# A third early block of deformable samples, a denser second layer, and an addition and a copy on other engines

## The chip, the core and the metric

The kernel runs on one core of one Trainium2 chip. The metric is the time of one execution on the device, in microseconds, as the median of several runs.

## The reference, cut to what matters

Four layers are computed in turn on an input of 2 images (batches) of 256 channels and 64 x 64 pixels:

```
x = attention(group_norm(x)): 4 heads, q.k over all 4096 pixels, softmax, times v,
    projection, plus the normalized x
x = x + position term
x = bottleneck(x): 1x1 convolution to 64 channels, deformable 3x3 convolution
    (offsets and a mask from a 3x3 convolution; each of 9 taps is a bilinear
    sample at its own place), 1x1 convolution to 256 channels, plus x
x = x + two times: group_norm, relu, deformable 3x3 convolution over 256 channels
    (offsets from a 7x7 depthwise and a 1x1 convolution)
```

A bilinear sample is a gather of four neighbouring pixels, weighted. Everything is float32.

## The kernel before, in words

The pixels of a batch are tiled into 8 blocks of 512 (`NB`). The order of the work on TensorE, ScalarE, VectorE and GpSimd (POOL in the profile) is the order in which the program issues it; the DMAs of SyncE (SP) are placed by the framework. The program has two parts.

**Attention** (line 181 on) goes through 4 units, a batch and a pair of heads each. A unit has 16 blocks of 256 queries, a block 16 positions `n`, so there are 1024 positions; the main loop (line 677) makes two of them per turn. For each it multiplies queries and keys (line 580), takes the maxima on VectorE (592), the exponentials on ScalarE (598), turns them on TensorE (610), copies the turned halves out of PSUM on VectorE or ScalarE (`keep`, line 617) and multiplies with the values (639). At the end of a block the softmax shares of its parts are turned and sent through DRAM (`spread`, line 499: a store to `share_d` and two loads of `f`), and GpSimd merges the parts with them (`combine`, 514). The next block's first product is copied into the same tile `o` (471).

What else is to be done runs in the background, as generators. `background(count)` (line 661) goes down their list and makes up to `count` productive steps. It is called for each position that has no step of the attention's own (`small`, 691) and once more at the end of a turn (724). The list holds, in turn: the bottleneck's first layer and offsets (`before`, 954); for batch 0 within units 2 and 3 its second layer (`conv`, 1041), which has 144 steps of two gathers on POOL, a product on VectorE (1065) and two additions (1075, 1076; on POOL for batch 0, on VectorE for batch 1), with transposes, matmuls and copies between; then `early_image` (1178), which normalizes the result and writes the image `img3` that deform gathers from; and in unit 3 `early_samples` (1215). The latter computes the offsets for the first `EARLY` blocks of deform. Each block has 36 gathers (9 taps, 4 groups of 128 pixels); `gather` (1254) issues them one by one on POOL, 11 per 16 positions, and stores each gathered tile of 128 x 1024 to `samp_d` by SP.

**Deform** (line 1299) computes both deformable layers of both batches: 4 x 8 blocks of 36 steps `s`. A step gets its gathered tile (`gather`, 1437, called 8 steps ahead), weighs its first corner on ScalarE (1459), adds the other three on VectorE (1465), turns the sample on TensorE (1477), and every four steps it is copied (1486) and multiplied (1496). For the first `EARLY` blocks of batch 0 the tiles are read from `samp_d` by SP (the first 8 by POOL) and no offsets are computed; for all others POOL gathers.

Beside the steps run `Side` generators with a rate of calls per step: the second layer of batch 1 (`seconds`, 0.9 a step and 2.5 more for each step of the early blocks), after its end the image of batch 1 (0.9 a step; it first loads batch 1 by SP into the memory that the second layer used), and the offsets of later blocks (24 per 36 steps, begun 58 steps before block `EARLY`):

```
offs = [Side(EARLY * BLOCK - LEAD - 6, OFFS / BLOCK, begun)]
seconds = Side(0, 0.9, second, lambda s: 2.5 * min(s, EARLY * BLOCK))
```

`corners` (731) turns offsets into indices and weights with small VectorE operations; its tiles come from the pool that it is given.

Of the kernel before, what the change touches and what calls it, by code (L numbers as in the profile page):

```python
# [11 lines left out]
F32 = mybir.dt.float32  # L12
BF16 = mybir.dt.bfloat16
I32 = mybir.dt.int32
# [6 lines left out]
P = 128  # L21
# [4 lines left out]
K2 = 9  # L26
EPS = 1e-5
DWK = 7

EARLY = 2  # L30


GH, GW = H + 1, W + 2
# [31 lines left out]
class Net:  # L65
# [115 lines left out]
    def attention(self, bott):  # L181
# [4 lines left out]
        tc, nc, a = self.tc, self.nc, self.a  # L186
        with ExitStack() as ctx:
# [58 lines left out]
            q, k, v = {}, {}, {}  # L246
# [370 lines left out]
            def keep(n, pts, engine):  # L617

                u, i, c, t, h = parts(n)
                if n % 4 == 0 and n // 4 not in ets:  # L620
                    ets[n // 4] = etp.tile([P, 8, 2, 256], F32, name="et")
                for j, pt in enumerate(pts):
                    at = P * t + 64 * j
                    dst = ets[n // 4][:, :, h, at : at + 64]
                    if j and (u < 2 or h == 0 or t):
                        if engine == "DVE":
                            nc.vector.tensor_copy(dst, pt)  # L627
                    elif engine == "ACT":
                        nc.scalar.copy(dst, pt)  # L629
# [31 lines left out]
            def background(count):  # L661
                for g in list(back):
                    while count:
                        r = next(g, None)
                        if r is None:
                            back.remove(g)
                            break
                        if not r:
                            break
                        count -= 1  # L670
# [6 lines left out]
            while n < last + 4 or back or more or any(own.values()):  # L677
                u, d = divmod(n, per_unit)
                if d == 0 and u < len(units):
                    plan_unit(u)  # L680
                    if u == 0:
                        back.append(prepare(1))
                    if u == 1:
                        back.append(bott.before(0, bt, ps))
                    if u == 2:
                        back.append(first_batch())
                    if u == 3:
                        back.insert(0, bott.before(1, bt, ps))
                        back.append(self.early_samples(bott, bt, held, xp, vp, kp, ps))

                def small(at):
                    steps = own.pop(at, ())
                    for f in steps:
                        f()
                    if not steps and u > 1:
                        background(1)

                if n - 1 in pts:
                    p = pts.pop(n - 1)
                    keep(n - 1, p, "ACT")  # L700
                    keep(n - 1, p, "DVE")
                ps.flush()
                sc = [scores(m) for m in (n + 2, n + 3) if m < last]
                for m in range(len(sc)):
                    lowest(n + 2 + m, sc[m])
                if n < last:
                    p = turn(e.pop(n))
                    keep(n, p, "DVE")
                if sc:
                    e[n + 2] = exponentials(n + 2, sc[0])  # L710
                if n < last:
                    keep(n, p, "ACT")

                small(n)
                if 4 <= n < last + 4:
                    attend(n - 4)
                    attend(n - 3)
                small(n + 1)
                if n < last:
                    pts[n + 1] = turn(e.pop(n + 1))  # L720
                if sc:
                    e[n + 3] = exponentials(n + 3, sc[1])
                if u or n % 8 == 0:
                    background(1)

                for _ in range(1 + (n % 16 in (10, 12, 14))):
                    more = self.sample()
                n += 2


    def corners(self, i, pt, mask, base, idx, w4, pool):

        nc = self.nc
        p = pool.tile([P, 4, K2, 2], F32, name="pos")
        off = pt[:, :, 0 : 2 * K2].rearrange("p j (k t) -> p j k t", t=2)
        nc.vector.tensor_tensor(p, off, base[:, 4 * i : 4 * i + 4], ALU.add)
        if mask:
            mk = pool.tile([P, 4, K2], F32, name="mask")  # L740
            nc.vector.tensor_scalar_max(mk, pt[:, :, 2 * K2 : 3 * K2], -87.0)
        yield False
        if mask:

            nc.scalar.activation(mk, mk, AF.Exp, scale=-1.0)

        nc.vector.tensor_scalar(p, p, float(H), -1.0, ALU.min, ALU.max)
        whole = pool.tile([P, 4, K2, 2], I32, name="whole")
        nc.vector.tensor_copy(whole, p)
        yield True  # L750
        f = pool.tile([P, 4, K2, 2], F32, name="floor")
        nc.vector.tensor_copy(f, whole)
        g = pool.tile([P, 4, K2, 2], F32, name="above")
        nc.vector.tensor_tensor(g, f, p, ALU.is_gt)
        yield False
        nc.vector.tensor_tensor(f, f, g, ALU.subtract)
        nc.vector.tensor_scalar_min(f, f, float(H - 1))
        w = pool.tile([P, 2, 4, K2, 2], F32, name="wt")
        nc.vector.tensor_tensor(w[:, 1], p, f, ALU.subtract)
        yield False  # L760
        nc.vector.tensor_scalar(w[:, 0], w[:, 1], -1.0, 1.0, ALU.mult, ALU.add)
        at = pool.tile([P, 4, K2], F32, name="at")
        nc.vector.scalar_tensor_tensor(
            at, f[:, :, :, 0], float(GW), f[:, :, :, 1], ALU.mult, ALU.add
        )
        nc.vector.tensor_scalar_add(idx, at, float(GW + 1))
        yield True
        if mask:
            nc.vector.tensor_scalar_add(mk, mk, 1.0)
            nc.vector.reciprocal(mk, mk)  # L770
            yield False
            for s in range(2):
                nc.vector.tensor_mul(w[:, s, :, :, 1], w[:, s, :, :, 1], mk)
            yield False
        for s in range(4):
            nc.vector.tensor_mul(w4[:, :, :, s], w[:, s % 2, :, :, 0], w[:, s // 2, :, :, 1])
        yield True
# [76 lines left out]
    class Bottleneck:  # L854
# [44 lines left out]
        def pools(self, ctx, gathers=5):  # L899
            self.ahead = gathers - 1  # L900
            tc = self.net.tc
            return self.kept | {
                n: ctx.enter_context(tc.tile_pool(name=f"bt_{n}", bufs=bufs))
                for n, bufs in (("g", gathers), ("s", 8), ("t", 6), ("x", 2))
            }

        def block(self, pool, src, i):
# [133 lines left out]
        def conv(self, b, pools, ps):  # L1041
# [28 lines left out]
            def add(n, four, sampled):  # L1070

                i, g, js = steps[n]
                engine = (nc.gpsimd, nc.vector)[b]
                sm = pools["s"].tile([P, 2, CM], F32, name="bsmp")
                engine.tensor_add(four[:, :, 0:2, :], four[:, :, 0:2, :], four[:, :, 2:4, :])  # L1075
                engine.tensor_add(sm, four[:, :, 0, :], four[:, :, 1, :])
                if g < 4:
                    sampled.append(sm.rearrange("p n f -> p (n f)"))
                else:
                    sampled.extend(sm[:, m, :] for m in range(2))  # L1080
# [218 lines left out]
    def deform(self, bott):  # L1299
# [5 lines left out]
        with ExitStack() as ctx:  # L1305
            gp = ctx.enter_context(tc.tile_pool(name="df_g", bufs=10))
            wp = ctx.enter_context(tc.tile_pool(name="df_w", bufs=1))
            work = ctx.enter_context(tc.tile_pool(name="df_work", bufs=2))
            cp = ctx.enter_context(tc.tile_pool(name="df_c", bufs=4))
            sp = ctx.enter_context(tc.tile_pool(name="df_s", bufs=5))  # L1310
            tp = ctx.enter_context(tc.tile_pool(name="df_t", bufs=2))
            pmisc = ctx.enter_context(tc.tile_pool(name="df_pm", bufs=1, space=PSUM))
# [88 lines left out]
            def offsets(b, l):  # L1401
                if b == 0:
                    yield from offset_weights(l)
                wf = self.wf
                for i in range(EARLY if (b, l) == (0, 0) else 0, NB):
                    idx = cp.tile([P, 4, K2], I32, name="didx")
                    w4 = cp.tile([P, 4, K2, 4], F32, name="dw4")
                    corners[b, l, i] = idx, w4
                    yield from self.offsets(
                        i,  # L1410
                        [x[b][:, cb, :] for cb in range(2)],
                        lambda s, row: wf[:, s, DWK * row : DWK * row + DWK, :].rearrange(
                            "p t o -> p (t o)"
                        ),
                        self.vec[:, V_PWB + l : V_PWB + l + 1],
                        base, idx, w4, work, ods[i % 2], pd,
                    )

            ods = [wp.tile([P, 8, W + DWK - 1], F32, name=f"wide{n}") for n in range(2)]
# [284 lines left out]
```

## Time and profile before

| | us |
|---|---|
| median of 3 runs | 5151.03 |
| lowest and highest run | 5145.72, 5154.88 |
| span of the profiled execution, first to last instruction | 5149.0 |
| attention's units 0 to 3, from the first maximum of each | 59, 740, 1450, 2189 |
| deform's first weighed sample | 2995 |

The profiled execution is one run of its own. Its own time is its span, 5149.0 us, with what lies around the first and last instruction, which the profile doesn't give; the span lies within the range of the runs, 2.0 us under their median. The profile names an engine's work by line, tile and operation; a busy time is a union over instructions, and idle time is put down to what ended it.

### The profile page before, as it was taken

The numbers are of one execution on the slowest core, as the hardware profiler recorded it, in microseconds if no ns is written. First come the engines' busy times: TensorE is split into PE (matmuls) and PEld (weight loads), VectorE is DVE, ScalarE is ACT, GpSimd is POOL, SyncE is SP. The second block draws the span as 40 slices with busy tenths as digits, with TensorE's granted clock in tenths as the row PEclk, the third lists the DMA queues.
The fourth block names the chain that finished last, engine by engine and source line by source line (L and its number), as shares of the span: only waits on it lengthen the run. The fifth ranks groups of instructions, "written<-read, shape, count | busy, mean of one in ns | idle before, by whom it ended". The sixth has DMA issues, their size and how long they took to land. (4 is left out here: it accounts for less than half of the span.)

```text
span 5149.0 us, 100000 instructions
## 1 busy us (share of the span) xinstructions
PE 4816.8 (94%) x38200; PEld 2651.9 (52%) x38200; DVE 4196.7 (82%) x7929; ACT 2883.6 (56%) x5221; POOL 2254.7 (44%) x2256
## 2 busy tenths in 40 slices
PE   8999999999999999999999957679999999999998
PEld 5555565555565555565555523234444444444443
DVE  6878867878668888687766768878999999999998
ACT  5666656666666666666656622235444554454444
POOL 0111111111107777464023257775666566666665
PEclk9999999999999999999999967789999999999999
DMA  5231121111113333322557677679999999999998
GB/s 172 61 99 51 42 68 49 35 46 30 55 52 94 93 100 102 94 85 79 150 193 272 233 242 239 207 251 376 340 329 339 360 359 350 356 388 346 347 348 318
DMA packets 367022, 997.66 MB, mean 194 GB/s; under 512 B 61372, under 2 KB 98810, under 8 KB 366542
## 3 DMA queue, kind: packets, MB, share of 16 engines
q0 software_dynamic: 196560, 690.41, 37.7%
q1 hardware_dynamic: 169438, 300.73, 17.9%
q8 instruction: 300, 4.92, 0.4%
q14 instruction: 180, 1.47, 0.1%
q10 hardware_dynamic: 544, 0.13, 0.0%
HBM read 855.36 MB, written 127.35 MB: 191 GB/s over the span
## 5 line engine op out<-in xcount | busy, mean ns | idle before, releaser
L1465 DVE SCALAR_TENSOR_TENSOR smp<-four,dw,smp 128x256 f32<-128x256 f32 x3240 | 1503.8, 483 | 122.3 <-ACT smp L1459 44.4
L598 ACT ACTIVATE e<-sc,low 128x1024 f32<-128x1024 f32 x1024 | 1147.1, 1120 | 745.1 <-DVE low L592 741.4
L592 DVE TENSOR_REDUCE low<-sc 128x1 f32<-128x1024 f32 x1024 | 1204.8, 1218 | 228.1 <-PE sc L580 224.0
L846 POOL DMA_INDIRECT four<-img,didx x1080 | 1085.4, 1005 | 646.3 <-DVE smp L1465 349.2
L1496 PE MATMUL out<-st,wc 128*128 128x512 f32 x2304 | 1229.6, 616 | 65.0 <-ACT st L1486 33.6
L580 PE MATMUL sc<-k,qs 64*128 64x512 f32 x2048 | 997.1, 605 | 1.8 <-ACT e L598 1.4
L639 PE MATMUL av<-et,v 128*64 128x256 f32 x8192 | 996.5, 385 | 0.0
L580 PE MATMUL sc<-k,q 64*128 64x512 f32 x2048 | 977.3, 604 | 0.0
L519 POOL TENSOR_TENSOR o<-o,f 128x1024 f32<-128x1024 f32 x63 | 149.3, 2370 | 1771.5 <-DMA f<-share_d 890.1
L610 PEld LDWEIGHTS tt<-ident,e 64*128 64x128 f32 x16384 | 651.7, 139 | 519.3 <-issue 275.4
L1459 ACT ACTIVATE smp<-four,dw 128x256 f32<-128x256 f32 x1080 | 535.9, 507 | 594.3 <-PE pt L1477 460.4
L610 PE MATMUL tt<-ident,e 64*128 64x64 f32 x16384 | 726.1, 226 | 40.5 <-ACT et L629 19.9
L629 ACT COPY et<-tt 128x512 f32<-128x512 f32 x1152 | 659.5, 586 | 170.5 <-PE tt L610 169.2
L627 DVE COPY et<-tt 128x512 f32<-128x512 f32 x896 | 612.0, 683 | 161.3 <-PE tt L610 160.9
L639 PEld LDWEIGHTS av<-et,v 128*64 128x64 f32 x8192 | 552.1, 137 | 302.9 <-issue 48.4
L1477 PEld LDWEIGHTS pt<-ident,smp 128*128 128x128 f32 x2304 | 320.5, 144 | 740.8 <-issue 423.4
L846 POOL DMA_INDIRECT bfour<-img,bidx x576 | 581.0, 1009 | 184.2 <-issue 90.3
L1496 PEld LDWEIGHTS out<-st,wc 128*128 128x128 f32 x2304 | 392.0, 196 | 323.3 <-issue 216.5
L1477 PE MATMUL pt<-ident,smp 128*128 128x128 f32 x2304 | 454.6, 280 | 72.7 <-DVE smp L1465 67.1
L580 PEld LDWEIGHTS sc<-k,qs 64*128 64x128 f32 x2048 | 345.4, 188 | 215.7 <-issue 120.0
L1486 ACT COPY st<-pt 128x1024 f32<-128x1024 f32 x288 | 291.2, 1011 | 289.5 <-PE pt L1477 287.8
L803 PE MATMUL pd<-x,wf 128*126 128x512 f32 x840 | 433.4, 598 | 0.0
(183 smaller groups left out, 3600.4 us busy)
## 6 DMA issues: line engine op xcount, KB each, us to landing
f<-share_d SPq DMA_DIRECT2D x128, 256.0 KB
four<-samp_d SPq DMA_DIRECT2D x64, 512.0 KB
xb<-xn SPq DMA_DIRECT2D x55, 512.0 KB
img<-imgt SPq DMA_DIRECT2D x96, 256.0 KB
four<-img,didx POOLq DMA_INDIRECT x1080, 6.1
xa<-res SPq DMA_DIRECT2D x32, 512.0 KB
samp_d<-xb SPq DMA_DIRECT2D x32, 512.0 KB
xb<-in_x SPq DMA_DIRECT2D x20, 512.0 KB
```

What stands on the lines that cost most here:

```text
L580: nc.tensor.matmul(s[:, j, :], lhsT=q[u, i // 2][int(h != j)][halves[j], at : at + P], rhs=k[u][c][halves[j], h, :], start=True, stop=True,)
L592: nc.vector.tensor_reduce(low, s, AX.X, ALU.max, negate=True)
L598: nc.scalar.activation(e.rearrange("p j n -> p (j n)"), s, AF.Exp, bias=blk.low[:, g, c : c + 1], accum_out=blk.sum[:, g, c : c + 1],)
L610: nc.tensor.transpose(pt[:, m, :], e[half, m // 4, m % 4 * P : m % 4 * P + P], self.ident[half, half],)
L627: nc.vector.tensor_copy(dst, pt)
L629: nc.scalar.copy(dst, pt)
L639: nc.tensor.matmul(now["av"][halves[h], :], lhsT=v[u][c][:, m, halves[h]], rhs=ets[j][:, m, h, :], start=(m == 0), stop=(m == 7),)
L846: self.nc.gpsimd.indirect_dma_start(out=dst, out_offset=None, in_=img, in_offset=bass.IndirectOffsetOnAxis(ap=idx, axis=0),)
L1459: nc.scalar.mul(smps[s], fours[s][:, 0], weight(s, 0))
L1465: nc.vector.scalar_tensor_tensor(smps[s], four[:, c], weight(s, c), smps[s], ALU.mult, ALU.add)
L1477: nc.tensor.transpose(pts[u][:, c, j * P : (j + 1) * P], smp[:, c * P : c * P + P], self.ident,)
L1496: nc.tensor.matmul(outs[ob], lhsT=wc[k][:, c, ob * P : ob * P + P], rhs=sts[u][:, c, :], start=(k == 0 and c == 0), stop=(k == K2 - 1 and ...
```

## The change

`EARLY` becomes 3: a third block has its offsets computed, gathered and stored within the attention, and is read back in deform. In unit 2 one more of the turned halves' copies goes to ScalarE (positions with the second head and the second half of the queries; unit 3 is as it was). In units 2 and 3 every second turn makes two background steps at its end instead of one. The first of batch 0's two additions in the bottleneck's second layer is made on VectorE. To make room, `corners` uses one tile for three of its values, deform's corners come from a pool with one buffer, and the ring of bottleneck samples has 7 tiles instead of 8.

```diff
-EARLY = 2
+EARLY = 3
...
-                    if j and (u < 2 or h == 0 or t):
+                    if j and (u < 2 or h == 0 or t and u > 2):
...
                 if u or n % 8 == 0:
-                    background(1)
+                    background(1 + (u > 1 and n % 4 == 0))
...
-        whole = pool.tile([P, 4, K2, 2], I32, name="whole")
+        whole = pool.tile([P, 4, K2, 2], F32, name="whole").bitcast(I32)
...
-        g = pool.tile([P, 4, K2, 2], F32, name="above")
+        g = whole.bitcast(F32)
...
-        at = pool.tile([P, 4, K2], F32, name="at")
+        at = g.rearrange("p j k t -> p (j k t)")[:, : 4 * K2]
+        at = at.rearrange("p (j k) -> p j k", k=K2)
...
-                for n, bufs in (("g", gathers), ("s", 8), ("t", 6), ("x", 2))
+                for n, bufs in (("g", gathers), ("s", 7), ("t", 6), ("x", 2))
...
-                engine.tensor_add(four[:, :, 0:2, :], four[:, :, 0:2, :], four[:, :, 2:4, :])
+                nc.vector.tensor_add(four[:, :, 0:2, :], four[:, :, 0:2, :], four[:, :, 2:4, :])
...
+            once = ctx.enter_context(tc.tile_pool(name="df_k", bufs=1))
...
-                        base, idx, w4, work, ods[i % 2], pd,
+                        base, idx, w4, once, ods[i % 2], pd,
+                        odp=lambda: work.tile([P, 512], F32, name="od"),
```

## The prediction

> **What bounds the kernel now.** I read the page first, for the shape of the run.
>
> ```profile
> span 5149.0 us, 100000 instructions
> ...
> PE 4816.8 (94%) x38200; PEld 2651.9 (52%) x38200; DVE 4196.7 (82%) x7929; ACT 2883.6 (56%) x5221; POOL 2254.7 (44%) x2256
> ...
> POOL 0111111111107777464023257775666566666665
> ```
>
> TensorE is busy 94% on average, but the POOL slices show different stages. So I cut the span where they change. The columns are busy us (and instructions) of PE, PEld, DVE, ACT, POOL, then the granted clock, DMA share and GB/s.
>
> ```profile
> 1450.00:2189.00 739.00, 727.45 (x7908) 436.25 (x7906) 581.94 (x831) 493.02 (x920) 445.35 (x489) 1.00 0.31 90
> 2189.00:2975.00 786.00, 756.67 (x7865) 450.77 (x7863) 561.62 (x900) 509.63 (x947) 255.41 (x264) 0.99 0.50 166
> 3005.00:3300.00 295.00, 183.21 (x558) 84.57 (x559) 254.39 (x595) 66.60 (x123) 222.43 (x217) 0.75 0.72 234
> 3300.00:3460.00 160.00, 115.88 (x377) 55.11 (x376) 125.29 (x283) 46.49 (x82) 123.73 (x120) 0.84 0.70 223
> ...
> 3604.00:5100.00 1496.00, 1427.67 (x5123) 689.42 (x5122) 1401.55 (x3307) 737.07 (x1273) 935.66 (x934) 1.00 0.96 352
> ```
>
> Attention units 2 and 3 (first two rows) are TensorE's: 98% and 96% busy at full clock. Whatever is added to TensorE there is paid in full. From 3604 on, TensorE (95%), VectorE (94%) and the DMA engines (0.96) are all near their ends. In between, 3005 to 3460, nothing is full: TensorE 62%, VectorE 83%. The indirect gathers alone, by stage (POOL busy and count):
>
> ```profile
> 3005.00:3300.00 295.00, 222.43 (x217) 0.75 0.72 234
> 3300.00:3384.00 84.00, 64.80 (x64) 0.76 0.61 191
> 3384.00:3460.00 76.00, 58.93 (x57) 0.93 0.80 259
> ```
>
> 338 gathers in 455 us: one per 1.35 us, about 1.0 busy plus 0.3 to issue, evenly in every slice. POOL's issue is the limit of this stage, with VectorE close behind. Of the 338, 288 are second-layer gathers of batch 1 and the rest are deform's own. How many deform steps pass meanwhile is seen from ScalarE's first product (line 1459), one per step:
>
> ```profile
> 3384.00:3460.00 76.00, 14.90 (x30) 0.93 0.80 259
> 3460.00:3604.00 144.00, 37.56 (x76) 0.96 0.97 370
> 3604.00:3704.00 100.00, 31.56 (x63) 1.00 0.94 342
> ```
>
> With the steps before 3384 counted on the same line, deform stands at step 89 at 3384, at 119 at 3460 and at 195 at 3604. It then takes 1.59 us a step (57 us a block of 36).
>
> **Does the third block fit into attention?** I walked the background calls through the loop. Outside the unit changes, before makes 33 productive calls per 32 positions in unit 2 and after 41. Batch 0's second layer starts near position 546 in both and drains at 842 before, 780 after. The early image follows (852 to 886 before, 786 to 804 after). 72 gathers ran from position 902 to 1004; 108 would run from 812 to 968. The trace agrees for before: first such gather at 2614 us, last at 2913, attention's last exponential ends at 2966.8. So three blocks end 56 positions ahead of the end: no tail is added.
>
> **Attention, part by part.**
>
> *Third offset block.* Two blocks' matmuls in attention:
>
> ```profile
> L803 PE MATMUL pm<-v,bx 128*126 128x512 f32 (+3 forms) x56 | 23.3, 573 | 0.0
> ...
> L823 PE MATMUL pm<-k,shift 126*32 126x512 f32 x28 | 3.9, 602 | 0.0
> L837 PE MATMUL pm<-sel,bst 128*128 128x32 f32 x16 | 2.2, 279 | 0.0
> ```
>
> 29.4 us for two, so +14.7 us on a full TensorE. Removing it from deform saves nothing by itself: block 2's offsets lie in the POOL-limited stage.
>
> *36 more gathers, stores and the SP queue.* A store of samples waits on SP for its gather, and the shares that the attention's merge needs stand behind it:
>
> ```profile
> 2790.38 6.23 SPq L1259 DMA_DIRECT2D samp_d<-xb  x3
> 2792.32 0.27 DVE L504 COPY shares<-pm 16x128 f32<-16x128 f32 x1
> ...
> 2799.20 0.38 SPq L506 DMA_DIRECT2D share_d<-shares  x1
> ...
> 2808.57 2.34 POOL L519 TENSOR_TENSOR o<-o,f 128x1024 f32<-128x1024 f32 x1 [21.27 <-DMA f<-share_d]
> ...
> 2813.08 0.42 DVE L471 COPY o<-av 128x256 f32<-128x256 f32 x1 [6.17 <-POOL avs L525]
> ...
> 2814.16 1.03 PE L610 MATMUL tt<-ident,e 64*128 64x64 f32 x15 [4.55 <-DVE et L627]
> ```
>
> The shares were ready at 2792.6, left at 2799.2, and TensorE lost 4.55 us at the end of the chain (another 3.77 at 2903). 8.3 us for 72 gathers is +4.2 for 36 (0 to 10).
>
> *Denser steps.* The second layer's and the image's TensorE work is only moved within attention: 0. At the image's new pace (8 blocks in 18 positions, about 6.5 us each) ScalarE may wait for a block's load. Before, the closest pair of blocks was 7.3 us apart and the wait 1.03 us. I take +2 (0 to 8).
>
> *First addition to VectorE, copy to ScalarE.* For unit 2 between 1500 and 2180 (105 products at line 1065) VectorE gains 105 additions of 0.422 (its price in batch 1's rows, 777 ns on POOL), 25 more products with additions of 1.20, and 6 us of what follows them: +80 us. It loses 64 copies of 0.683: -44. Net +36 on 540, so 79% becomes about 84%; ScalarE gets 64 x 0.586 = +38 us, 67% to 72%. TensorE was 99.8% busy in 100 to 200 us with VectorE at 85%, so I take 0 here (-3, since TensorE waited 3.1 us on these copies, to +13, 0.1 us in each of 128 iterations). The Trainium skill speaks against the move: "SBUF — State Buffer", SBUF: two separate sides, says a VectorE instruction with two SBUF inputs and a GpSimd instruction that reads SBUF exclude each other for a whole instruction. The row of the neighbouring product agrees: 669 to 2356 ns, median 682, mean 779 over the run. By the rule at its worst each of 144 additions waits out a whole 2.37 us merge: 341 us. By the row the mean excess is 0.1 us: 14 us of VectorE time, hidden. I take the row; the change also takes 144 x 0.777 = 112 us of GpSimd reading away. On POOL only the second addition now waits for VectorE, with later gathers behind it; the gathers run four steps ahead.
>
> *Smaller rings.* With 7 instead of 8 sample tiles, an addition takes over the tile of one step later. In the timeline the transposes that free it end at least 3.9 us before that addition in batch 0 and 2.0 in batch 1: 0. The single-buffered corner tiles in deform and the shared tile for floor and index are VectorE's alone, in order: 0.
>
> Attention: 14.7 + 4.2 + 2 = +21, less 2 for the copies = **+19 us** (+8 to +40).
>
> **Deform.** The second batch's layer goes at 0.9 calls per step plus 2.5 for the early ones, about 301 calls in all. Before it gets 3.4 a step to step 72, then 0.9, and ends at step 134. After it keeps 3.4 and ends at step 88. Until then POOL has only its 288 gathers: at one per 1.32 us (every 50 us slice from 3050 to 3450 holds 38) they end at 3005 + 288 x 1.32 = 3384. So both kernels stand near step 89 at 3384. Before still has 27 second-layer gathers and pays 2.5 us a step to 119; after has none, nor own gathers until block 3. From there batch 1's image runs (some 52 calls at 0.9, 58 steps) in both. I price steps 89 to 147 by the row in which before did that, 144/76 = 1.89 us: 110 us. Then 48 steps at 1.59 = 76. After reaches step 195 at 3384 + 186 = 3570, before at 3604: -34 us.
>
> Here another rule of the skill speaks against it: "DMA: Bandwidth & Descriptors", Issuing engines are not separate DMA queues, says all issuers share the same engines and another issuer saves issue time only. If bytes were the limit, 36 extra stores and reads of 512 KB would make it a loss: 38 MB at the 350 GB/s of the last row is 108 us of DMA. But the row has the DMA share at 0.72 and gathers at one constant interval, so issue time is the limit, and 36 x 1.32 = 48 us of it leave the stage. The stores fall where the share is 0.50.
>
> *SP queue.* Reads of steps 97 to 107 now pass SP near the load of batch 1's image. In before that load waited on SP for memory from 3463.3 to 3500.5 and again 11 us for a store, with nothing urgent behind. Reads go 8 steps (15 us) ahead, so 11 us plus a landing of 7.3 exceed that by 3. I take +3 (0 to 29).
>
> Deform: **-31 us** (-42 to -3).
>
> **Sum.** 5149.0 + 19 - 31 = 5137 of span; the median stands 2 us above the span of the profiled execution: **5139**.
>
> **Rivals.** (1) *The reads are held on SP.* If the image load blocks SP as long as in before, 37.2 us, and step 97's reads stand behind it, deform stalls 37.2 + 7.3 - 15 = 29 us instead of 3: 5165, slower. It decides from 16 us of stall on. For: the wait is in the trace. Against: before's wait began only because nothing else was queued. Chance 0.24 (with the dearer ends of attention). (2) *VectorE and the gather stage eat it.* 0.1 us in each of unit 2's 128 iterations, 13 us: 5152. Against: 85% with TensorE full. Chance 0.24. (3) *Attention hardly loses.* Unit 3's stall of some 11 us, where image and batch 1's first layer overlap, goes: 5128. Chance 0.10. (4) *It does not fit*, and gathers trail attention: excluded by 56 positions. The forecast has 0.42.
>
> This kernel's measurement can tell about 0.2% (10 us) from no change. (3) and the forecast are faster: 0.52; (2) same: 0.24; (1) slower: 0.24. The range runs from the low ends of deform with little attention cost, 5112, to a little over (1), 5168.
>
> **What would show it.** Attention's end later by about 19 us, unit 2 longer and unit 3 shorter than the 739 and 786 us of before (second-layer work moves forward); first early gather 70 us or more sooner; POOL's even row of gathers ending near 3384 + 19; step 195 about 12 us earlier than 3604; the last 26 blocks at 57 us. Wrong if TensorE's idle time in unit 2 rises, if reads of samples land late near step 97, or if deform's early steps cost other than 4.5 us.

## The result, and the profile after

The changed kernel takes 5202.61 us (median of 4 runs, 5199.2 to 5205.97) and the kernel before, run with it, 5148.38 us (5144.68 to 5154.88). The ratio is 1.0104, with an interval of 1.009 to 1.0118: 54 us slower, where the forecast stood 12 us under the 5151 us known then. The prediction was wrong in sign, and the time is above the upper end of its range, 5168 us.

The page of the changed kernel, the same rows as for before:

```profile
span 5198.0 us, 100239 instructions
...
PE 4833.6 (93%) x38200; PEld 2658.7 (51%) x38200; DVE 4229.8 (81%) x8009; ACT 2915.1 (56%) x5285; POOL 2149.5 (41%) x2112
...
POOL 0111111111116766521323147755666566666665
```

TensorE has as many matmuls as before (38200) and is busy 17 us longer, while the span has grown by 49. The work did move as the prediction walked it. The second layer's slices (the 7s and 6s) are shorter and start in the same place, and the early gathers come sooner: first at 2403 us (2614 before), last at 2880, with the last maximum of attention at 3023. The third block fits.

Where the time went is seen from three marks. Attention's units 0 and 1 last 680.5 and 710.3 us (before 680.9 and 710.7). Unit 2 lasts 780.5 (before 738.7), and unit 3 with what follows it, up to deform's first weighed sample, 827.0 (before 806.4). Deform lasts 2141.9 (before 2153.6). So attention's last two units are 62 us longer (what comes before them is 2 us shorter, so deform starts 61 us later), and deform is 12 us shorter. Units 2 and 3 in the cut by windows (columns as before: busy us and instructions of PE, PEld, DVE, ACT, POOL, then granted clock, DMA share, GB/s):

```profile
1448.00:2222.00 774.00, 737.89 (x7910) 443.25 (x7908) 632.69 (x937) 526.50 (x987) 443.32 (x467) 0.99 0.32 97
2229.00:3023.00 794.00, 753.15 (x7730) 443.73 (x7728) 537.20 (x870) 501.00 (x929) 187.36 (x175) 0.98 0.57 201
```

TensorE is 95% busy in both, where before it was 98% and 96%: it now waits about 36 us in the first window and 41 in the second (12 and 29 before), and its clock is a little lower. The prediction had named this itself as a sign of being wrong: TensorE's idle time in unit 2 rises. No other engine is full: VectorE has 82% and 68%. What TensorE waits for is best seen at one of the gaps. This is the timeline of unit 2 around 1846 us (start, duration, engine, line, tiles; in brackets the idle time before and what ended it):

```profile
1839.45 2.37 POOL L519 TENSOR_TENSOR o<-o,f 128x1024 f32<-128x1024 f32 x1
1840.29 1.83 DVE L1076 TENSOR_TENSOR bfour<-bfour 128x256 f32<-128x256 f32 x1
...
1842.04 1.49 DVE L1128 TENSOR_SCALAR bx<-bx,bn_t 128x512 f32<-128x512 f32 x1
...
1844.07 2.35 POOL L527 TENSOR_TENSOR res<-res,pos 128x1024 f32<-128x1024 f32 x1
1844.17 2.80 DVE L1066 TENSOR_TENSOR bfour<-bfour,bw 128x512 f32<-128x512 f32 x1
...
1847.49 2.34 DVE L592 TENSOR_REDUCE low<-sc 128x1 f32<-128x1024 f32 x2
...
1848.80 1.11 ACT L598 ACTIVATE e<-sc,low 128x1024 f32<-128x1024 f32 x1 [5.82 <-DVE low L592]
...
1850.53 1.12 PE L610 MATMUL tt<-ident,e 64*128 64x64 f32 x16 [4.42 <-ACT et L629]
```

Read it backwards. TensorE waited 4.42 us. The last releaser is ScalarE's copy `et`, but ScalarE itself had waited 5.82 us for the maxima (line 592), and the maxima stood on VectorE behind a row of background work: the new first addition (1076), the end of a second-layer block (1128, 1129) and a product (1066). Three of them are drawn out (1.83, 1.49 and 2.80 us, where the medians of these lines are 0.42, 0.48 and 0.68), and GpSimd was at the merge meanwhile (519 to 527, from 1839.5 to 1846.4). VectorE runs in program order, so work that "only moves" sits in front of the next maxima.

### The profile page after: what moved, and what is told of

Its sections match the earlier page's. It is cut to its first block, busy times and chain, and to the rows that moved or that the text cites. A ratio compares the mean times of both kernels' runs of the same rounds, so it can differ in the third digit from the quotient of the medians.

```text
span 5198.0 us, 100239 instructions
## 1 busy us (share of the span) xinstructions
PE 4833.6 (93%) x38200; PEld 2658.7 (51%) x38200; DVE 4229.8 (81%) x8009; ACT 2915.1 (56%) x5285; POOL 2149.5 (41%) x2112
## 3 DMA queue, kind: packets, MB, share of 16 engines
q14 instruction: 182, 1.49, 0.1%
## 5 line engine op out<-in xcount | busy, mean ns | idle before, releaser
L1468 DVE SCALAR_TENSOR_TENSOR smp<-four,dw,smp 128x256 f32<-128x256 f32 x3132 | 1450.2, 483 | 99.4 <-ACT smp L1462 24.4
L847 POOL DMA_INDIRECT four<-img,didx x1044 | 1046.6, 1003 | 674.9 <-DVE smp L1468 353.5
L1462 ACT ACTIVATE smp<-four,dw 128x256 f32<-128x256 f32 x1044 | 517.6, 507 | 508.6 <-PE pt L1480 483.6
L629 ACT COPY et<-tt 128x512 f32<-128x512 f32 x1216 | 690.5, 586 | 159.8 <-PE tt L610 158.5
L627 DVE COPY et<-tt 128x512 f32<-128x512 f32 x832 | 569.1, 684 | 153.8 <-PE tt L610 150.4
L804 PE MATMUL pd<-x,wf 128*126 128x512 f32 (+3 forms) x812 | 412.5, 590 | 0.0
```

What stands on the lines that cost most here:

```text
L804: nc.tensor.matmul(pd[:m, r0 * W : r1 * W], lhsT=wt(s, t), rhs=src[:, (y + r0 - y0) * W : (y + r1 - y0) * W], start=(n == 0), stop=(n == l ...
L847: self.nc.gpsimd.indirect_dma_start(out=dst, out_offset=None, in_=img, in_offset=bass.IndirectOffsetOnAxis(ap=idx, axis=0),)
L1468: nc.vector.scalar_tensor_tensor(smps[s], four[:, c], weight(s, c), smps[s], ALU.mult, ALU.add)
```

## The experiments

All kernels compute everything. Each edit is against the changed kernel unless it says otherwise. The groups ran at different times. The kernel before, run beside each, took 5147.06 and 5149.94 us in the first two groups, 5312.83 in the third and 5347.0 in the fourth; the cause is open (the first group and the fourth carry the same chip number). So only ratios, and differences within one group, are compared; runs of the first two groups are also set beside the changed kernel's 5202.61 us, since the kernel before took 5148.38 us there.

### First group: the addition, the steps, the merge

**The first addition back on GpSimd:**

```diff
-                nc.vector.tensor_add(four[:, :, 0:2, :], four[:, :, 0:2, :], four[:, :, 2:4, :])
+                engine.tensor_add(four[:, :, 0:2, :], four[:, :, 0:2, :], four[:, :, 2:4, :])
```

> The changed kernel, with the first of batch 0's two additions back on GpSimd (its place before). Changed kernel: 5203, unit 2 of attention 773 us, unit 3 794. Theory L (lockout): the merge of a block on GpSimd shuts out VectorE's two-input instructions (first additions 0.42 us alone, 0.93 beside GpSimd), and the maxima behind them come late; without the additions unit 2 falls to about 755 and the kernel to about 5185. Theory D (density): three calls instead of two and a half a turn are too many, whoever adds; VectorE loses 144 x 0.42 = 61 us, but GpSimd at 144 x 0.78 more becomes late with gathers: unit 2 stays within 770 to 785, the kernel within 5195 to 5215. Theory T (third block alone costs it): no change, 5203.

Measured: 5216.79 us, 1.0132 (1.0116 to 1.0149); unit 2 lasts 794.1 us. It became 14 us slower, not faster. TensorE's waits changed kind. Up to position 752, the gaps that end at the attention's own work, with a copy of turned halves, fall from 27.5 us in the changed kernel to 11.0: with less in VectorE's queue the maxima come earlier. But 30.6 us (7.4 in the changed kernel) now end at a matmul of the background work, which mostly waits for the samples that GpSimd adds. So the addition on VectorE is not the culprit by itself; within the denser steps it helps.

**Single steps with three blocks:**

```diff
-                    background(1 + (u > 1 and n % 4 == 0))
+                    background(1)
```

> The changed kernel with one background step at the end of each turn again, as before (third block, addition and copy stay). By the walk through the loop the third block's gathers then end some 32 positions behind the last one, so a tail of about 25 to 35 us is added to attention. Theory L: most of the stall stays, since every addition still meets the merge: unit 2 about 755 (less second-layer work in it: 739 plus some 15), kernel about 5205 to 5220. Theory D: the stall of both units goes: unit 2 about 739, the kernel 5203 - 40 + 30 = about 5193. Theory T: 5203 + 30 = 5233.

Measured: 5223.43 us, 1.0148 (1.0131 to 1.0165). Unit 2 falls to 732.3 us, 48 less, so the denser steps are what makes unit 2 long. But the kernel isn't faster: the third block no longer fits, and deform's first sample comes 83 us after the last maximum (2978 to 3061), against 33 in the changed kernel. The denser steps, at least those of unit 2, are needed for the third block and are too dear for it.

**The merge on VectorE in unit 2**, so that GpSimd and VectorE no longer meet there (the addition of the position term likewise):

```diff
-        engine = nc.vector if end else nc.gpsimd
+        engine = nc.vector if end or self.u == 2 else nc.gpsimd
-        nc.gpsimd.tensor_add(self.res, self.res, self.pos)
+        engine.tensor_add(self.res, self.res, self.pos)
```

> The changed kernel with the merge of a block of queries (line 519 to 527) on VectorE instead of GpSimd in unit 2 alone; everything else as in the changed kernel. VectorE gets some 16 x 2.9 us more, and no merge is left that shuts it out. Theory L: unit 2 falls from 773 to about 758, the kernel to about 5188. Theory D (VectorE simply has too much to do): unit 2 rises by 10 to 45 us, the kernel to 5213 to 5245. Theory T: no change in unit 2.

Measured: 5208.52 us, 1.0121 (1.0104 to 1.0138); unit 2 782.8. Nothing is won. In the gap shown above the two engines seem to get in each other's way, but taking that away by giving VectorE the merge leaves unit 2 as long. But this run also adds the merge to VectorE's own work, so it can't tell what the meeting alone costs: the one may have taken the other's place.

**Denser steps in unit 2 alone** (`u > 1` becomes `u == 2` in the same line):

> The changed kernel with the second background step in unit 2 alone; unit 3, where the early image and the third block are, has single steps as before. The third block still fits: the image ends near position 812 instead of 804. Theory D: the image's compressed pace costs unit 3 about 15 to 20 of its stalls, so the kernel falls to about 5185, unit 3 from 794 to about 777. Theory L: the image's steps hold few two-input instructions of VectorE: unit 3 within 5 us of 794, the kernel 5198 to 5206. Theory T (gathers and offsets of the third block): no change, 5203.

Measured: 5192.67 us, 1.0086 (1.0069 to 1.0103), 10 us less, though the intervals overlap; unit 2 781.6, unit 3 812.3 instead of 827.0. What the pace costs in unit 3 is separate, smaller, and needless for the third block, which still fits.

### Second group: the copies, and the block apart from the steps

**The copy back on VectorE, and all these copies of unit 2 on ScalarE:**

```diff
-                    if j and (u < 2 or h == 0 or t and u > 2):
+                    if j and (u < 2 or h == 0 or t):
```

```diff
-                    if j and (u < 2 or h == 0 or t and u > 2):
+                    if j and u != 2 and (u < 2 or h == 0 or t):
```

> The changed kernel with unit 2's copy back on VectorE (as before). Theory V (VectorE late in a dense unit 2: its maxima come late, then the exponentials, then the copies): 44 us more on VectorE, unit 2 rises from 780 to 790 or more, kernel 5212 to 5225. Theory S (two copies in a row on ScalarE hold TensorE's next turning, as the waits for line 629 say): unit 2 falls to about 760, kernel about 5183.

> The changed kernel with all copies of turned halves on ScalarE in unit 2: 128 more leave VectorE (87 us), 75 us come to ScalarE (67% to 77%). Theory V: TensorE's idle time in unit 2 falls from 36 to 15 or less, unit 2 from 780 to about 760, kernel about 5182. Theory S: more copies in a row on ScalarE, unit 2 rises to 795 or more, kernel 5217 or more.

Measured: 5219.92 us, 1.0137 (1.012 to 1.0154), unit 2 796.7; and 5221.68 us, 1.0139 (1.0122 to 1.0156), unit 2 795.4. Both directions lose about 15 us. Neither "VectorE is too full" nor "ScalarE is too full" alone can be the theory: up to position 752, VectorE and ScalarE are busy 87% and 63% in the first and 74% and 75% in the second (84% and 69% in the changed kernel), and the loss is the same. With the first addition's run, this makes three moves of work between the engines, and each lengthens unit 2 by 14 to 16 us. In the last of these runs TensorE's idle time in unit 2 isn't higher (34.5 us against 36.1), so it shows the price but not its place.

**The change with two blocks** (`EARLY = 2`), **and that with single steps as well** (which leaves the addition, the copy and the memory edits):

> The changed kernel with two early blocks: third block undone, the dense steps, the addition, the copy and the smaller tiles stay. If the third block is worth its while in deform (forecast: 19 us of attention for 31 of deform) the kernel is slower than the changed one: 5215. If the changed trace reads right (15 to 20 us of attention for 12 of deform): unit 3 falls by about 19, deform rises by 12, kernel 5194 to 5200; the dense steps then carry nearly the whole loss.

> The changed kernel with two early blocks and single background steps: what is left of the change is the addition on VectorE, the copy on ScalarE and the smaller tiles. The run with single steps and three blocks had unit 2 at 732 against 739 before. If that gain is the addition's and the copy's and the tiles cost nothing: kernel 5147 - 6 = 5141, faster than both. If the smaller rings cost something after all, 5150 or more.

Measured: 5199.55 us, 1.0097 (1.008 to 1.0114) with two blocks; 5154.47 us, 1.0008 (0.9999 to 1.0017) with single steps too. These two settle most of it. They differ in the denser steps alone, and that is 45 us of the 54. Units 2 and 3 with single steps:

```profile
1449.00:2174.00 725.00, 714.14 (x7822) 432.06 (x7818) 582.00 (x867) 517.92 (x972) 362.05 (x378) 1.00 0.31 91
2181.00:2961.00 780.00, 753.94 (x7804) 448.39 (x7802) 574.91 (x927) 505.26 (x940) 228.72 (x229) 0.99 0.50 167
```

and with denser ones, both with two blocks:

```profile
1448.00:2222.00 774.00, 737.87 (x7918) 443.74 (x7916) 632.02 (x936) 525.25 (x984) 443.40 (x467) 0.99 0.34 97
2229.00:3003.00 774.00, 738.27 (x7712) 438.33 (x7710) 534.83 (x854) 500.19 (x927) 154.50 (x141) 0.98 0.47 157
```

Unit 2 has about 90 more matmuls and 70 more VectorE instructions and grows by 48 us (732.6 to 780.7); unit 3 has as many fewer matmuls and shrinks by only 4. Work was moved, but TensorE's time was not: unit 2's row goes from 98.5% busy to 95.3%. VectorE's busy share of that row rises only from 80% to 82%.

The cost can be added up from TensorE's side. From unit 2's first maximum to deform's first sample its idle time goes from 47 us to 82 (+35), and the time at half clock within the two units from 20.5 us to 44.4. If half of the latter 24 is lost, 12 us, the two make an estimate of 47, for the 44 us by which the units grew.

### Third group: parts alone

**The addition and the copy alone, and the memory edits alone**, each put into the kernel before (the diffs are those of the change):

> The kernel before with the first addition on VectorE and the copy on ScalarE, nothing else (two early blocks, single steps, eight sample tiles). Unit 2 was 6 us shorter with them in the run with two blocks and single steps, but deform 5 us longer. If the smaller tiles cost those 5 us: 5150 - 6 = 5144. If addition and copy are worth nothing by themselves: 5150.

> The kernel before with the smaller memory alone: one tile for floor and index, deform's corners from one buffer, seven sample tiles. Forecast: no cost, 5150. If deform's 5 us more came from here: 5155.

Measured: ratios of 0.9999 (0.999 to 1.0008) and 1.0011 (0.9999 to 1.0023). Neither has a cost or a gain that can be measured. The first is notable beside the first two groups: the same two edits are worth some 15 us each within the denser steps and nothing measurable without them.

**The extra step off the turn of the merge**, in both units and in unit 2 alone (`u == 2`):

```diff
-                    background(1 + (u > 1 and n % 4 == 0))
+                    background(1 + (u > 1 and n % 16 in (0, 8, 12, 14)))
```

> The changed kernel with the extra background step in the turns at 0, 8, 12 and 14 of each 16 positions instead of 0, 4, 8 and 12: as many steps, none in the merge's turn. Theory M (the steps pile up on VectorE in the merge's turn: 23 of the 35 us of TensorE's gaps lie in the turn after it): unit 2 from 780 to about 758, the clock's halved stretches with them, kernel 5175 to 5185. Theory D (the number of steps alone): unit 2 within 775 to 785, kernel 5198 to 5207.

> As the run with the extra step off the merge's turn, and only in unit 2. Theory M with the run that was dense in unit 2 only (10 to 15 us less in unit 3): kernel 5165 to 5175. Theory D: 5190 to 5195. It would beat the kernel before only if unit 3 lost nothing, which neither expects.

Measured: 1.0036 (1.0022 to 1.0049) and 1.0029 (1.002 to 1.0039). It looked like most of the loss was gone, but the changed kernel itself had not run beside these two. So it ran again beside its mends.

### Fourth group: the mends beside the changed kernel

The changed kernel again; the extra step off the merge again; the second layer's high rate in deform only up to step 84, so that its end isn't hurried (`lambda s: 2.5 * min(s, 84)` in place of `min(s, EARLY * BLOCK)`); and three mends in one (unit 2 only, off the merge, slow end).

> The changed kernel itself, beside the next three on the same chip, since the last runs met a chip on which the kernel before took 5313. On a chip like the first: 5203, ratio 1.010. On one like the last: what the ratio of the two then is shows whether the run off the merge's turn (1.0036 there) gained anything.

> The changed kernel with as many extra background steps, none in the merge's turn. Theory M (they pile up on VectorE in the merge's turn): 18 to 28 us under the changed kernel of the same chip. Theory D (their number alone): within 5 us of it. The last trace of this kernel had unit 2 at 787 with gaps of 17 us still in the turn at 6, so I expect less than M's full size, about 5 to 15 us.

> The changed kernel with the second batch's second layer at its high rate to step 84 instead of 108, so that its last 16 calls come at 0.9 a step. In the changed trace steps 88 to 96 take 44 us where 15 were forecast, at the end of that layer. If its last chain (turn, copy, matmul, activation, matmul, addition) is exposed by coming in two steps: deform falls from 2142 by 10 to 20 us, kernel about 15 under the changed one. If the load of batch 1's image on SyncE holds the third block's reads: the slow steps move with the layer's end or stay, and the kernel is within 5 us.

> The three mends together: extra steps in unit 2 only and none in the merge's turn, and the slow tail. If they add up: 10 to 15 from unit 3, 5 to 15 from the merge's turn, 10 to 20 in deform, so 25 to 50 under the changed kernel: 5153 to 5178, at best level with the kernel before.

| | median, us | ratio | interval | unit 2 | unit 3 | deform |
|---|---|---|---|---|---|---|
| changed again | 5401.34 | 1.011 | 1.0085 to 1.0136 | 805.0 | 869.5 | 2272.7 |
| off the merge | 5395.16 | 1.0092 | 1.0067 to 1.0117 | 790.0 | 874.3 | 2279.2 |
| slow end | 5393.45 | 1.009 | 1.0066 to 1.0114 | 811.5 | 869.2 | 2264.8 |
| three mends | 5375.78 | 1.0056 | 1.0037 to 1.0074 | 793.9 | 857.5 | 2282.3 |

The changed kernel's ratio is the same in this slower group (1.011 for 1.0104). Off the merge, unit 2 becomes 15 us shorter, but the total gains only 6, which the intervals don't resolve; the third group's 1.0036 for the same kernel did not come back. The merge's turn is part of the loss in unit 2, not the whole: TensorE's gaps behind it fall from 26 to 16 us. With the slow end, steps 88 to 96 of deform take 20 us instead of 44, and step 108 comes 527 us after deform's start instead of 541. But only 8 of these 14 us are left at the end, hardly more than the 6.5 by which two kernels with the same deform differ here (2272.7 and 2279.2). With the three mends the same steps also take 20 us, and deform is not shorter at all (2282.3). So a gain from the slow end is not shown. The three together win 26 us, by their traces in units 2 and 3 (23 us shorter), and still leave the kernel 0.6% over the one before. No version that I ran beats it.

## Why the prediction was wrong, step by step

**It fits.** Right: the walk's margin was 56 positions, and the last early gather began 143 us ahead of the last maximum.

**"The second layer's and the image's TensorE work is only moved within attention: 0", and "so I take 0 here" for VectorE.** This is the step that failed, by some 42 us: the denser steps were put at 0 for TensorE's work and 2 us for a load, with VectorE's part called hidden, and the two runs with two blocks show 44. The TensorE work was indeed only moved, and the first addition and the copy by themselves do cost nothing measurable (ratio 0.9999). But the sum for VectorE also held the 25 products that the denser steps bring, and I had judged it by the busy share (79% to about 84%; measured up to position 752, 82% and 84%) and by another stage, 100 to 200 us, where TensorE was 99.8% busy beside a VectorE at 85%. There 74 of VectorE's 85 us were maxima and turned copies, an even stream of one position after the other. In unit 2 background steps come in bursts in front of the maxima, and a burst of two steps can put several us of products, additions and block ends into the one queue that feeds the exponentials. The loop makes the exponentials three positions ahead at most, and that is the margin, not the average. The second rival (VectorE eats it, 13 us by 0.1 us in each iteration) had the right side and the wrong form: the loss isn't spread. Of the 35 us of TensorE gaps in unit 2 up to position 752, 23 lie in one of the eight turns, that at position 6, behind the merge (0.4 of 11 before); it lasts 6.97 us on average, 5.27 before.

The gap shown above is the rule in that turn. Of its twelve gaps of over 0.7 us, eleven, 20 us of the 23, lead back the same way: ScalarE waited 2.2 to 5.8 us for maxima that stood on VectorE behind products and first additions, mostly three of them. Here is VectorE ahead of the gap of 2.23 us that ends at 1800.2:

```profile
1792.27 2.40 DVE L1076 TENSOR_TENSOR bfour<-bfour 128x256 f32<-128x256 f32 x1
1794.60 1.75 DVE L1066 TENSOR_TENSOR bfour<-bfour,bw 128x512 f32<-128x512 f32 x1
1796.38 0.83 DVE L1076 TENSOR_TENSOR bfour<-bfour 128x256 f32<-128x256 f32 x1
1797.14 2.34 DVE L592 TENSOR_REDUCE low<-sc 128x1 f32<-128x1024 f32 x2
```

and in the kernel with single steps and two blocks, ahead of a gap of 1.60 us, the longest of this turn there:

```profile
1732.36 2.63 DVE L1076 TENSOR_TENSOR bfour<-bfour 128x256 f32<-128x256 f32 x1
1734.92 1.76 DVE L1066 TENSOR_TENSOR bfour<-bfour,bw 128x512 f32<-128x512 f32 x1
1736.60 2.34 DVE L592 TENSOR_REDUCE low<-sc 128x1 f32<-128x1024 f32 x2
```

The first two are as slow there, but the third is missing; the gaps of this turn are 7 us in all, and those of unit 2 up to position 752 are 10.

**The Trainium skill's rule on the two sides of SBUF** ("SBUF — State Buffer", SBUF: two separate sides: the two engines exclude each other for a whole instruction). I took the row's mean excess against its worst case, 14 us of VectorE time. In units 2 and 3 the first additions that run beside a GpSimd operation other than a gather take 0.934 us (40 of 144), the others 0.419, together 21 us more, which agrees with the rule in kind and is far from its worst case. The size was about right, and "hidden" was half wrong. The exclusion alone doesn't carry the loss: with single steps an addition beside the merge is as slow (2.63 us in the rows above), and TensorE's gaps are 10 us instead of 35. But in the gap above an addition and a product beside GpSimd's work took 1.83 and 2.80 us, right in front of maxima.

```profile
L1076 DVE TENSOR_TENSOR bfour<-bfour x128: 402/424/2629, 1555.8 to 2149.0; 128x256 f32<-128x256 f32 x128
```

This row of the changed kernel between 1500 and 2150 us (shortest, median and longest in ns) shows why a mean misled: the median is that of an addition alone, and the longest is six times it.

**Third block: +14.7, +4.2 and +2 us.** Nearly right. Two blocks against three, all else equal, is 23 us of attention (unit 3 with its tail 804.0 to 827.0), forecast 21. The mend for unit 2 alone shows that unit 3's length with three blocks also depends on the pace there (812.3).

**Deform: −31 us, measured −12.** The mechanism was right and two terms were mis-sized. Against the two-block run the third block does take 19 us (2161.3 to 2141.9); that run is itself 8 us longer here than the kernel before, and why was not looked into. The gathers of batch 1's second layer run at the one even interval that I used:

```profile
3065.00:3200.00 135.00, 100.56 (x99) 0.68 0.72 245
3200.00:3360.00 160.00, 123.75 (x120) 0.73 0.72 238
3360.00:3445.00 85.00, 65.81 (x64) 0.80 0.70 232
```

(POOL, line 847, of the changed kernel: 283 gathers in 380 us, 1.34 each.) They end 389 us after deform's start, as forecast (3384 − 2995). But the last gather is not the end of the layer. Here are the windows after it:

```profile
3445.00:3474.00 29.00, 17.93 (x49) 7.18 (x48) 19.43 (x49) 5.62 (x12) 7.54 (x8) 0.62 0.40 128
3474.00:3490.00 16.00, 12.63 (x31) 5.70 (x30) 11.88 (x39) 6.17 (x10) 0.00 (x0) 0.77 0.90 325
3490.00:3514.00 24.00, 21.55 (x81) 11.17 (x80) 18.78 (x41) 10.16 (x19) 8.92 (x9) 1.00 1.02 392
```

and how many deform steps pass in them (ScalarE, line 1462, one product a step):

```profile
3436.00:3490.00 54.00, 5.78 (x12) 0.71 0.62 210
3490.00:3514.00 24.00, 5.78 (x12) 1.00 1.02 392
```

For 54 us a step takes 4.5 us, and in the next row 2.0. In the 54 us no compute engine is near its end, and the clock is at 0.62 and 0.77. Up to 3474 it is the layer's last calls (turn, copy, matmul, activation, matmul, addition), which still come at 3.4 a step: each waits for the one before (ScalarE's copies 19 us in all for the turns, an addition 7.0 us for its matmul), and the deform steps stand behind them in each engine's order. Then the image of batch 1 begins, and ScalarE waits 3.8 us for its norm and 5.8 for its load. I had priced steps 88 to 96 at 1.89 us, 15 in all; they took 44. After that the steps were cheaper than I priced them, 1.75 for 1.89 us up to step 147 and 1.57 for 1.59 up to step 195, which gives 8 back. So 29 lost and 8 won turn the −34 that I had worked out for step 195 (without the 3 us for the SP queue) into −13. The run with the slow end bears out that the rate of the calls makes these steps slow (20 us instead of 44), but what is left of it at the end of deform is too little to be told from chance.

**The first rival (reads held on SP), 29 us.** Not seen at that size: from 3490 to 3700 us a deform sample waits for a read once, for 6.7 us. Its total of 5165 was nearer to the result than my forecast, by luck: the loss lies elsewhere.

**Sum.** Forecast +19 − 31 = −12 us of span; measured +61 − 12 = +49. In parts, units 2 and 3 take +44 for the denser steps, +23 for the third block and −4 for the rest of the change (1540.9 us with two blocks and single steps, 1545.1 before).

What stays open: how the 44 us of the denser steps divide between the number of steps in a burst and their place in the block. Off the merge's turn unit 2 gave back 15 us, the rest wasn't taken apart.

## What to carry to other kernels

A busy share is no slack when the work arrives in bursts in front of a step with a deadline: ask what stands in that engine's queue ahead of the instruction that feeds the bound engine, turn by turn, before you call a move free. When work is brought forward to make room for more, price both: here the third block alone broke even (+23 and −19 us), and the pace that it needs cost 45. And the end of a pipelined side job isn't its last transfer: price its closing chain of dependent steps too.

## What the runs showed of the hardware

TensorE's short gaps cost more than their length. After the 4.42 us gap shown above (1846.1 to 1850.5) the granted clock is halved for 6.8 us; the windows of the changed kernel:

```profile
1846.50:1849.90 3.40, 0.00 (x0) 0.00 (x0) 3.37 (x5) 1.10 (x2) 2.80 (x4) 1.00 0.63 177
1849.90:1856.70 6.80, 6.17 (x44) 3.67 (x46) 5.11 (x8) 4.61 (x11) 5.00 (x6) 0.50 0.71 242
1856.70:1860.00 3.30, 3.30 (x36) 1.90 (x34) 1.97 (x5) 2.12 (x4) 1.91 (x3) 1.00 0.16 42
```

A matmul of the scores takes 1.06 us in the middle row and 0.59 otherwise. The Trainium skill ("TensorE: Matmul & The Clock Gate", Part 1: The HAM clock gate) says that the clock halves after an idle window of about 3.4 us. The stretches here last 3.4 or 6.8 us, one or two such windows; but gaps of 2.45 us (at 1945.1) and 2.46 us (at 2041.9), shorter than a window, were followed by one too. The length of a gap alone doesn't decide it: two of 2.23 us in unit 2 were not followed by one, and one of 2.25 us in unit 3 (at 2335.6) was. In unit 2 there were 17.1 us at half clock, and none before.

An edit's worth was not the same each time. For one kernel (the extra step off the merge's turn) the ratio to the kernel before was 1.0036 (1.0022 to 1.0049) where the latter took 5312.83 us, and 1.0092 (1.0067 to 1.0117) where it took 5347.0, so a mend has to be run beside what it mends.
